# Row sums of layer 1 on GpSimd, norm statistics under the score products, the last biases in a convolution's sums

## The chip, the cores and the metric

The kernel runs on one core of a Trainium2 chip (trn2). The metric is the device time of one execution in microseconds. Times without a profile are from plain runs; the profile comes from one execution of its own, which takes a little longer, and its records are what the views below are made from.

## The reference

Two attention blocks stand one after the other on eight images of 512 channels by 32 x 32 pixels, all in fp32. Block 0 has 8 heads of 64 channels, block 1 a single head of 512 channels. A group norm stands before each block (32 groups and 8 groups), a residual sum behind it. Cut to what matters:

```python
# x: (8, 512, 32, 32) -> per image 512 channels x 1024 tokens
h = group_norm(x, gn_weight, gn_bias)                 # block 0, 32 groups
qkv = einsum('oc,bct->bot', w_qkv, h) + b_qkv
q, k, v = 8 heads of 64 channels each
weight = softmax(einsum('bct,bcs->bts', q * s, k * s), axis=-1)
a = einsum('bts,bcs->bct', weight, v)
x = x + einsum('oc,bct->bot', w_proj, a) + b_proj

xn = group_norm(x, gamma, beta)                       # block 1, 8 groups
q, k, v = conv1x1(xn, q_w, q_b), conv1x1(xn, k_w, k_b), conv1x1(xn, v_w, v_b)
attn = softmax(einsum('bqc,bck->bqk', q, k) / sqrt(512), axis=-1)
out = einsum('bqk,bkc->bqc', attn, v)
x = x + conv1x1(out, p_w, p_b)
```

## The kernel before

**Algebra.** Once, at the start, the kernel multiplies block 1's weights together: `m` from its q and k weights, `z` from its v and projection weights. Block 1 then needs one convolution with `m` (its result is called g), scores g times h, and a by-token product with `z`. Most matrix products are done in Winograd's form of Strassen's scheme: operands are cut into quarters, sums of quarters ("factors") are made on VectorE or GpSimd, TensorE does seven products in place of eight, and the results are put together with a few adds. `left_sums` and `right_sums` make the factors; `ORDER` is 1, 5, 2, 6, 7, 3, 4. Block 1's scores and the convolutions of `k`, `q` and `m` use the scheme twice, one inside the other: `inner_factors` and `query_factors` make the inner factors on GpSimd.

**One inner product.** `inner_steps` runs the seven inner products, its steps, in the order 1, 6, 2, 5, 7, and leaves steps 3 and 4 in the list `tail`, which runs (through `finish`) after step 1 of the next product. Each step is a small burst of matmuls into one of three pools of PSUM banks a, b and c, two buffers each. After step 1 ScalarE copies psa into psb. Step 6 leaves u2 (printed u), step 5 leaves c5 (printed c), and steps 2, 7, 3 and 4 end in an add by `add` on VectorE that reads PSUM and writes a quarter of the result. If a product is the first to write its quarters, ScalarE copies in place of some of these. After each step one item of the list `background` is put into the program, more at other places. TensorE's instructions, and others under `keep_in_program_order`, stay in the order in which the program gives them; the rest is ordered by the scheduler, engine by engine. Each engine then works through a queue of its own in order, and waits at an instruction until all that it needs is there.

**The order of work.** For each image b: attention of block 0 (`attention0`), its projection with the residual sum (`projection`), then block 1 of the image before: `layer1_scores` (the convolution with `m`), `layer1_rest` (scores, z, values), then values, keys and queries of image b+1 for block 0. Block 1 of images 0 to 6 takes the scores with inner factors (`scores1_twice`); the last image takes `scores1`, which is not touched. One such round takes some 355 us.

**The convolution, `conv2`.** Four pairs of outer products: (1, 5), (2, 6), (7), (3, 4), each with its seven inner steps. `blocks` names quarters of the result by (row, column). `add` puts a PSUM bank into one or two quarters. In the pair with product 7 `more` adds quarters on GpSimd. `biased_half` adds the bias to a quarter with two ACTIVATEs of ScalarE; it runs for (0, 0) after pair 1, for (1, 1) after pair 2, and for (1, 0) and (0, 1) after pair 3, or, for `q`, in the list `late`, which the main loop puts under the attention that follows. A `k` convolution has no bias here.

**The scores, `scores1_twice`.** Seven outer products, numbered 0 to 6 here as in the code (they are products 1, 2, 5, 6, 7, 3, 4 of the scheme). The scores are kept in eight tiles `e`, by column c, half cc and row r. Outer product 4 (number 7 of the scheme) belongs to three quarters: its steps put PSUM into one quarter, and `more` adds quarters to each other on GpSimd, eight adds of 128x512 elements (line 715). When a quarter is complete, `exps` takes its exponential on ScalarE, 128x1024 elements at a time (line 719). `add_up` sums exponentials for the softmax: `parts[r]` gets the sum over column and half, six adds of 128x1024 on VectorE (lines 724 and 726, printed sum<-e,e and sum<-sum,e), and `total` gets the sum of its two halves on GpSimd (line 727).

**Statistics.** `projection` leaves a list `stats` of twelve items: for each of the image's four x tiles two `bn_stats` on half a tile, 128x512 (line 98), and one `bn_aggr` (line 103). Four of its items go into `background` in the convolution of the image before (through a hook of pair 1), five at the start of outer product 0 of the scores, after g's first two sums (`gsteps`), the rest at outer product 2. The group means are needed in z (`norm_hooks`). All big tiles, x, e and the sums among them, come from one pool of 32 buffers, so when a tile is last read decides when a later load or a later tile can have its place.

Of the kernel before, what the change touches and what calls it, by code (L numbers as in the profile page):

```python
# [12 lines left out]
ALU = mybir.AluOpType  # L13
# [16 lines left out]
def two_attention_blocks_kernel(  # L30
# [41 lines left out]
    def pcols(name):  # L72
        i = 4 * PARAMS.index(name)
        return par[:, i : i + 4]
# [101 lines left out]
    def main_path(ctx):  # L176
# [318 lines left out]
            tail.extend([lambda: step(3), lambda: step(4)])  # L495
            tail.extend(final)

        def conv2(n, f, bias, name, hooks=(), after=(), late=None):

            out = channel_tiles(name)
            hooks = list(hooks)

            def blocks(places, r, cc):

                if len(places) == 2 and places[0][0] == places[1][0] and places[0][1] < places[1][1]:
                    t = out[2 * places[0][0] + r].rearrange("p (c q n) -> p c q n", c=2, q=2)  # L510
                    return [t[:, :, cc, :]]
                return [
                    out[2 * i + r].rearrange("p (c q n) -> p c q n", c=2, q=2)[:, c : c + 1, cc, :] for i, c in places
                ]

            def add(dst, ps, x):

                n = max(len(dst), len(x))
                for i in range(n):
                    d = dst[i] if len(dst) == n else dst[0][:, i : i + 1, :]  # L520
                    nc.vector.tensor_add(d, ps[:, i : i + 1, :] if n > 1 else ps, x[i] if len(x) == n else x[0][:, i : i + 1, :])  # L521
# [12 lines left out]

            def pair(s, products, y, x, final):
                w = weights2[s // 2][:, (0, 2, 0, 1)[s] :]

                def mm(ps, j, start):
                    for i, p in enumerate(products):
                        matmul(ps[:, i, :], w[:, i, j - 1, :], f[p][j], start=start and i == 0, stop=True, skip_group_check=True)  # L540

                def extra(r, cc, read, written):
                    if products == (7,):
                        if read:
                            more((0, 1), (0, 1), (1, 1), r, cc)
                        if written:
                            more((1, 1), (1, 0), (1, 1), r, cc)

                inner_steps(
                    f"{name}_{s}", s % 2, len(products), mm, add, lambda *at: blocks(y, *at), x and (lambda *at: blocks(x, *at)),  # L550
                    extra, hooks.pop(0) if hooks else (), final,
                )

            weights2 = [weight_part((n, 0))]
            pair(0, (1, 5), [(1, 0), (1, 1)], None, [])
            pair(1, (2, 6), [(0, 0), (0, 1)], [(1, 0), (1, 0)], [load_weight, lambda: biased_half(0, 0)])
            weights2.append(weight_part((n, 1)))
            pair(2, (7,), [(1, 0)], [(0, 1)], [lambda: biased_half(1, 1)])
            last = [lambda: biased_half(1, 0), lambda: biased_half(0, 1)]
            if late is not None:  # L560
                late += last
                last = []
            pair(3, (3, 4), [(0, 1), (1, 0)], [(0, 1), (1, 0)], [load_weight, *last, *after])
            return out


# [126 lines left out]
        def scores1_twice(b, f, gf, gsteps, first, uid, stats):  # L693
# [14 lines left out]
            def blocks(at, r, cc):  # L708
                return [e[at[1], cc, at[0]][:, :, ts(r, 2 * P)]]
# [1 line left out]
            def add(dst, ps, x):  # L711
                nc.vector.tensor_add(dst[0], ps, x[0])  # L712

            def more(dst, x, y, r, cc):
                nc.gpsimd.tensor_tensor(blocks(dst, r, cc)[0], blocks(x, r, cc)[0], blocks(y, r, cc)[0], ALU.add)  # L715

            def exps(r, c):
                for cc in (1, 0):
# [1 line left out]

            def add_up(r, c):

                if r == c:
                    return [lambda: nc.vector.tensor_add(parts[r], e[c, 0, r], e[c, 1, r])]
                return [
                    *(lambda cc=cc: nc.vector.tensor_add(parts[r], parts[r], e[c, cc, r]) for cc in range(2)),
                    lambda: nc.gpsimd.tensor_tensor(total[:, r, :], parts[r][:, 0, :], parts[r][:, 1, :], ALU.add),
                ]

            def product(s, p, y, x, before, small, after7=(), final=()):  # L730
                def mm(ps, j, start):
                    for i in range(2):
                        matmul(
                            ps[:, i, :], f[p][j][:, ts(i, P)], g2[p][j], start=start and i == 0, stop=True, skip_group_check=True
                        )

                def extra(r, cc, read, written):
                    if p == 7:
                        if read:
                            more((0, 1), (0, 1), (1, 1), r, cc)  # L740
                        if written:
                            more((1, 1), (1, 0), (1, 1), r, cc)

                inner_steps(
                    f"{uid}_{s}", s % 2, 2, mm, add, lambda *at: blocks(y, *at), x and (lambda *at: blocks(x, *at)),
                    extra, after7, final, [lambda: background.extend(small), *(lambda q=q: factors(q) for q in before)],
                )

# [242 lines left out]
        def keys_and_queries(b, f, norm, hooks):  # L991

            k = conv2("k", f, None, f"k0_{b}", hooks)
            hooks = [[all_background], [], []]
            if norm:
                hooks[1].append(lambda: norm.group_mean(acc_tile(f"gmean_0_{b + 1}")[:, :KC]))
                hooks[2].append(lambda: norm.affine(acc_tile(f"gvar_0_{b + 1}")[:, :KC]))
            late = []
            q = conv2("q", f, pcols("bq0"), f"q0_{b}", hooks, late=late)
            return q, k, late  # L1000

        def layer1_scores(b, hf, inner, hooks=()):
            if inner:
# [37 lines left out]
        for b in range(B):  # L1041
# [17 lines left out]

            if b > 0:  # L1060
                hf, t = image_factors(h, f"h1_{b - 1}", here)
                extra[0] += late
# [13 lines left out]
            if b > 0:  # L1076
# [14 lines left out]
                if b + 1 < B:  # L1091
                    hf, steps = image_factors(h, f"h0_{b + 1}")
                    background.extend(steps)
                    v, f, norm0 = values(b + 1, hf)
                    q, k, late = keys_and_queries(b + 1, f, norm0, ())
            elif B > 1:
                v, f, norm0 = values(1, hf, [[], [], [], [], [*steps[:7], scaled, steps[7]]])
                norm1, stats = projection(0, af, xt)
                hooks = norm_hooks(norm1, "1_0")
                hooks[0].append(lambda: background.extend(stats))  # L1100
                q, k, late = keys_and_queries(1, f, norm0, hooks)
            else:
                for f in (*steps[:7], scaled, steps[7]):
                    f()
# [209 lines left out]
```

## Time and profile before

| | |
|---|---|
| Median of three plain runs | 2902.51 us (2902.0 to 2902.94) |
| The profiled execution | 2908.49 us |
| Its span in the profile | 2906.6 us |
| Mean granted TensorE clock | 0.994 |
| TensorE matmuls (PE) busy | 2852.4 us, 98% |
| TensorE weight loads (PEld) busy | 1678.3 us, 58% |
| VectorE (DVE) busy | 2098.9 us, 72% |
| GpSimd (POOL) busy | 1018.8 us, 35% |
| ScalarE (ACT) busy | 953.8 us, 33% |
| DMA, mean over the span | 97 GB/s |

The span runs from the first to the last instruction of the profile; the execution's time has a little more around it. Weight loads lie under matmuls. In the views a line such as `psb L67 <- DVE e L712: 29.8, 21, 3.7` says that TensorE, at its instructions into psb of line 67, waited 29.8 us in all, 21 times and at most 3.7 us, for VectorE's instruction of line 712 with the output e. A line of a timeline gives the start in us from the start of the span, the time from start to end, the engine, the line of the code, the operation, its output and inputs by the program's names, and the tile; several of a kind in a row are drawn together (x4). Brackets at its end say how long the engine was kept waiting before it, and by whom. A line of windows gives a stretch of time, its length, and then, for TensorE's matmuls and loads, VectorE, ScalarE, GpSimd and SyncE, the busy us (and the number of instructions), and last TensorE's clock, the DMA engines' busy share and GB/s.

### The profile page before, as it was taken

To read this page: it belongs to the slowest core of one execution; us is meant where nothing else is said; L and a number is where in the kernel's file an instruction comes from. 1 tells how busy PE (TensorE), PEld (TensorE's weight loads), DVE (VectorE), ACT (ScalarE), POOL (GpSimd) and SP (SyncE) were. 2 spreads that over 40 slices of the span, in tenths; PEclk is the share of its full clock that TensorE was granted. 3 is DMA by queue.
4 is the path that set the end of the run, shared out by engine and by line. 5 is a ranking of instruction groups with operands and counts; after the bars stand their busy time and mean duration, and the time that the engine had idled before them with its cause. 6 is when DMAs were issued, how large, how long until landed. Compare 5 with 4: busy or idle time off the path is not lost.

```text
span 2906.6 us, 32039 instructions
## 1 busy us (share of the span) xinstructions
PE 2852.4 (98%) x11720; PEld 1678.3 (58%) x11720; DVE 2098.9 (72%) x2760; ACT 953.8 (33%) x1222; POOL 1018.8 (35%) x1068
## 2 busy tenths in 40 slices
PE   9999999999999999999999999999999999999998
PEld 5435636765367653767437674376733768347544
DVE  5587787667876678775787667877588775887654
ACT  1351453215522055221642216431163312633110
POOL 2113226532164322742227412365124551145200
PEclk9999999999999999999999999999999999999999
DMA  8722403133032221322212231122411224021201
GB/s 274 245 91 105 155 19 141 52 116 125 33 124 87 98 108 48 109 92 104 102 48 105 92 135 70 48 105 95 153 53 48 102 102 149 21 81 68 94 0 67
DMA packets 91595, 281.03 MB, mean 97 GB/s; under 512 B 10595, under 2 KB 36387, under 8 KB 82470
## 3 DMA queue, kind: packets, MB, share of 16 engines
q1 hardware_dynamic: 89638, 276.61, 26.2%
q10 hardware_dynamic: 1792, 2.29, 0.2%
q8 instruction: 95, 1.56, 0.2%
q14 instruction: 70, 0.57, 0.1%
HBM read 225.93 MB, written 52.93 MB: 96 GB/s over the span
## 4 chain that ended last, share of the span: by engine, by line
PE 90%; DVE 4%; POOL 3%; issue 1%; ACT 1%; DMA 0%; SPq 0%; DVEq 0%; POOLq 0%; ACTq 0%
PE sc L67 16%; PE av L67 15%; PE psb_av L67 5%; PE psa_av L67 4%; PE psc_av L67 4%; PE psb L67 4%; PE psb_z L67 3%; PE psb_p L67 3%; PE psb_v L67 3%; PE psb_k L67 3%; PE psb_g L67 2%; PE psb_q L67 2%; POOL e L715 2%; PE psa_p L67 2%; PE psa_z L67 2%; PE psc_v L67 2%
## 5 line engine op out<-in xcount | busy, mean ns | idle before, releaser
L617 DVE TENSOR_TENSOR sum<-sum,e 128x1024 f32<-128x1024 f32 x384 | 519.3, 1352 | 41.8 <-DVE sum L617 1.8
L613 ACT ACTIVATE e<-sc 128x1024 f32<-128x1024 f32 x512 | 476.8, 1053 | 72.2 <-PE sc L67 72.2
L67 PE MATMUL sc<-q,k 64*128 64x512 f32 x2048 | 458.4, 597 | 0.0
L67 PE MATMUL av<-e,v 128*64 128x512 f32 x2048 | 453.6, 596 | 0.0
L67 PEld LDWEIGHTS sc<-q,k 64*128 64x128 f32 x2048 | 193.5, 186 | 238.1 <-ACT e L613 105.2
L67 PEld LDWEIGHTS av<-e,v 128*64 128x64 f32 x2048 | 141.4, 137 | 304.3 <-issue 302.3
L580 POOL TENSOR_TENSOR all_recs<-all_recs,rc 128x256 f32<-128x256 f32 x72 | 63.6, 884 | 567.7 <-DVE rc L578 560.1
L636 POOL TENSOR_TENSOR a<-a,r 128x512 f32<-128x512 f32 x56 | 116.7, 2083 | 263.5 <-DMA r<-rows 258.7
L578 DVE RECIPROCAL rc<-sums 128x256 f32<-128x256 f32 x72 | 126.5, 1757 | 48.0 <-PE sums L67 26.9
L631 ACT COPY a<-av 128x512 f32<-128x512 f32 x64 | 37.4, 585 | 305.6 <-PE av L67 305.6
L526 POOL TENSOR_TENSOR k<-k,k 128x256 f32<-128x256 f32 x28 | 20.1, 726 | 319.7 <-DVE u_k L521 319.7
L615 DVE TENSOR_TENSOR sum<-e,e 128x1024 f32<-128x1024 f32 x64 | 78.4, 1225 | 59.6 <-ACT e L613 59.6
L67 PE MATMUL psa_av<-e,z 128*128 128x512 f32 x256 | 113.3, 596 | 0.0
L67 PE MATMUL psb<-inner,inner_h 128*128 128x256 f32 x392 | 106.5, 397 | 0.0
L140 ACT ACTIVATE h<-h,b,s 128x1024 f32<-128x1024 f32 x62 | 78.3, 1268 | 80.4 <-DMA h<-in_x 64.9
L411 POOL TENSOR_TENSOR inner_h<-h,inner_h 128x256 f32<-128x256 f32 x112 | 95.8, 858 | 2.2
L411 POOL TENSOR_TENSOR inner_h<-t_h 128x256 f32<-128x256 f32 x84 | 85.0, 1015 | 17.9 <-PE psc_av L67 15.4
L67 PEld LDWEIGHTS psb<-inner,inner_h 128*128 128x128 f32 x392 | 78.2, 200 | 11.5
L719 ACT ACTIVATE e<-e 128x1024 f32<-128x1024 f32 x56 | 58.4, 1055 | 77.4 <-POOL e L715 42.0
L67 PE MATMUL psb_g<-inner_h,w_m 128*128 128x256 f32 x294 | 75.2, 384 | 6.3 <-DVE u_g L521 6.3
L67 PEld LDWEIGHTS psa_av<-e,z 128*128 128x128 f32 x256 | 48.1, 190 | 57.2 <-issue 56.5
L715 POOL TENSOR_TENSOR e<-e,e 128x512 f32<-128x512 f32 x56 | 69.9, 1268 | 21.3 <-DVE u L712 19.7
(374 smaller groups left out, 5438.8 us busy)
## 6 DMA issues: line engine op xcount, KB each, us to landing
x<-in_x SPq DMA_DIRECT2D x36, 512.0 KB
h<-in_x SPq DMA_DIRECT2D x32, 512.0 KB
spill<-x SPq DMA_DIRECT2D x32, 512.0 KB
h<-spill SPq DMA_DIRECT2D x32, 512.0 KB
x<-spill SPq DMA_DIRECT2D x32, 512.0 KB
out<-x SPq DMA_DIRECT2D x64, 256.0 KB
w_p<-sums_p SPq DMA_DIRECT2D x8, 1792.0 KB
r<-rows SPq DMA_DIRECT2D x112, 128.0 KB
```

The costliest lines, as they stand in the source:

```text
L67: tc.keep_in_program_order(nc.tensor.matmul(*args, **kw))
L140: tc.keep_in_program_order(nc.scalar.activation(dst, src, AF.Identity, bias=b, scale=s))
L411: pin(nc.gpsimd.tensor_tensor(dst, x, y, ALU.subtract))
L578: nc.vector.reciprocal(rc, sums)
L580: nc.gpsimd.tensor_tensor(all_recs, all_recs, rc, ALU.add)
L613: nc.scalar.activation(e, sc, AF.Exp, scale=(C // 8) ** -0.5)
L615: nc.vector.tensor_add(total, es[0], e)
L617: nc.vector.tensor_add(total, total, e)
L631: nc.scalar.copy(dst, av)
L636: nc.gpsimd.tensor_tensor(dst, dst, r, ALU.mult)
L715: nc.gpsimd.tensor_tensor(blocks(dst, r, cc)[0], blocks(x, r, cc)[0], blocks(y, r, cc)[0], ALU.add)
L719: nc.scalar.activation(e[c, cc, r], e[c, cc, r], AF.Exp, scale=scale)
```

## The change

It has four parts.

**Biases.** The halves (1, 0) and (0, 1) of a biased convolution (`q` and `m`) are no longer biased by ScalarE after pair 3. The adds of pair 3 that write them become a `scalar_tensor_tensor` each (PSUM plus bias plus the old quarter). `late` is gone. The halves (0, 0) and (1, 1) stay with ScalarE.

**Row sums.** The six adds of `add_up` on e go from VectorE to GpSimd, and all sums are pinned to the order of the program on GpSimd.

**Adds of outer product 4.** Of the eight `more` adds of `scores1_twice` two go from GpSimd to VectorE: the read one at (r, cc) = (0, 1), and the written one at (1, 0).

**Statistics.** None is in the convolution with `m` any more. The twelve items stand in outer products 0 (three, ahead of g's first sums), 3 (three, behind the first row sum), 4 (one), 5 (three) and 6 (two, ahead of row sums).

```diff
@@ conv2
-        def conv2(n, f, bias, name, hooks=(), after=(), late=None):
+        def conv2(n, f, bias, name, hooks=(), after=()):
...
                     d = dst[i] if len(dst) == n else dst[0][:, i : i + 1, :]
-                    nc.vector.tensor_add(d, ps[:, i : i + 1, :] if n > 1 else ps, x[i] if len(x) == n else x[0][:, i : i + 1, :])
+                    psi = ps[:, i : i + 1, :] if n > 1 else ps
+                    xi = x[i] if len(x) == n else x[0][:, i : i + 1, :]
+                    if isinstance(d, tuple):
+                        d, oc = d
+                        nc.vector.scalar_tensor_tensor(d, psi, bias[:, oc : oc + 1], xi, ALU.add, ALU.add)
+                    else:
+                        nc.vector.tensor_add(d, psi, xi)
...
             def pair(s, products, y, x, final):
+                def written(r, cc):
+                    to = blocks(y, r, cc)
+                    if s < 3 or bias is None:
+                        return to
+                    return [(t, 2 * i + r) for t, (i, _) in zip(to, y)]
...
-            last = [lambda: biased_half(1, 0), lambda: biased_half(0, 1)]
-            if late is not None:
-                late += last
-                last = []
-            pair(3, (3, 4), [(0, 1), (1, 0)], [(0, 1), (1, 0)], [load_weight, *last, *after])
+            pair(3, (3, 4), [(0, 1), (1, 0)], [(0, 1), (1, 0)], [load_weight, *after])
@@ scores1_twice
-            def more(dst, x, y, r, cc):
-                nc.gpsimd.tensor_tensor(blocks(dst, r, cc)[0], blocks(x, r, cc)[0], blocks(y, r, cc)[0], ALU.add)
+            def more(engine, dst, x, y, r, cc):
+                engine.tensor_tensor(blocks(dst, r, cc)[0], blocks(x, r, cc)[0], blocks(y, r, cc)[0], ALU.add)
...
             def add_up(r, c):
+                on = lambda dst, x, y: lambda: tc.keep_in_program_order(nc.gpsimd.tensor_tensor(dst, x, y, ALU.add))
                 if r == c:
-                    return [lambda: nc.vector.tensor_add(parts[r], e[c, 0, r], e[c, 1, r])]
+                    return [on(parts[r], e[c, 0, r], e[c, 1, r])]
                 return [
-                    *(lambda cc=cc: nc.vector.tensor_add(parts[r], parts[r], e[c, cc, r]) for cc in range(2)),
-                    lambda: nc.gpsimd.tensor_tensor(total[:, r, :], parts[r][:, 0, :], parts[r][:, 1, :], ALU.add),
+                    *(on(parts[r], parts[r], e[c, cc, r]) for cc in range(2)),
+                    on(total[:, r, :], parts[r][:, 0, :], parts[r][:, 1, :]),
                 ]
...
                         if read:
-                            more((0, 1), (0, 1), (1, 1), r, cc)
+                            more(nc.vector if (r, cc) == (0, 1) else nc.gpsimd, (0, 1), (0, 1), (1, 1), r, cc)
                         if written:
-                            more((1, 1), (1, 0), (1, 1), r, cc)
+                            more(nc.vector if (r, cc) == (1, 0) else nc.gpsimd, (1, 1), (1, 0), (1, 1), r, cc)
...
-            product(0, 1, (1, 0), None, [2], gsteps[:2] + stats[:5])
+            product(0, 1, (1, 0), None, [2], stats[:3] + gsteps[:2])
             product(1, 2, (0, 0), (1, 0), [5], gsteps[2:4], (), [lambda: exps(0, 0)])
-            product(2, 5, (1, 1), None, [6, 4], gsteps[4:] + stats[5:])
-            product(3, 6, (0, 1), (1, 0), [7, 3], add_up(0, 0))
-            product(4, 7, (1, 0), (0, 1), [], [])
-            product(5, 3, (0, 1), (0, 1), [], [], [lambda: exps(1, 1)], [lambda: exps(0, 1)])
+            product(2, 5, (1, 1), None, [6, 4], gsteps[4:])
+            product(3, 6, (0, 1), (1, 0), [7, 3], add_up(0, 0) + stats[3:6])
+            product(4, 7, (1, 0), (0, 1), [], stats[6:7])
+            product(5, 3, (0, 1), (0, 1), [], stats[7:10], [lambda: exps(1, 1)], [lambda: exps(0, 1)])
             product(
-                6, 4, (1, 0), (1, 0), [], add_up(1, 1) + add_up(0, 1), (),
+                6, 4, (1, 0), (1, 0), [], stats[10:] + add_up(1, 1) + add_up(0, 1), (),
                 [lambda: exps(1, 0), lambda: background.extend(add_up(1, 0) + steps)],
             )
@@ main loop
-                gf, gsteps = layer1_scores(b - 1, hf, inner, [[], [lambda: background.extend(stats[:4])]])
+                gf, gsteps = layer1_scores(b - 1, hf, inner)
...
-                layer1_rest(b - 1, hf, inner, gf, gsteps, stats[4:], [[], mean, [], affine], ahead)
+                layer1_rest(b - 1, hf, inner, gf, gsteps, stats, [[], mean, [], affine], ahead)
```

More of the change, by code (lines that the diff above doesn't have):

```diff
@@ L540, in mm, with extra @@
                         matmul(ps[:, i, :], w[:, i, j - 1, :], f[p][j], start=start and i == 0, stop=True, skip_group_check=True)
-                def extra(r, cc, read, written):
+                def extra(r, cc, read, done):
                     if products == (7,):
@@ L545, in extra @@
                             more((0, 1), (0, 1), (1, 1), r, cc)
-                        if written:
+                        if done:
                             more((1, 1), (1, 0), (1, 1), r, cc)
                 inner_steps(
-                    f"{name}_{s}", s % 2, len(products), mm, add, lambda *at: blocks(y, *at), x and (lambda *at: blocks(x, *at)),
+                    f"{name}_{s}", s % 2, len(products), mm, add, written, x and (lambda *at: blocks(x, *at)),
                     extra, hooks.pop(0) if hooks else (), final,
@@ L997, in keys_and_queries @@
                 hooks[2].append(lambda: norm.affine(acc_tile(f"gvar_0_{b + 1}")[:, :KC]))
-            late = []
-            q = conv2("q", f, pcols("bq0"), f"q0_{b}", hooks, late=late)
-            return q, k, late
+            q = conv2("q", f, pcols("bq0"), f"q0_{b}", hooks)
+            return q, k
         def layer1_scores(b, hf, inner, hooks=()):
@@ L1061, in main_path @@
                 hf, t = image_factors(h, f"h1_{b - 1}", here)
-                extra[0] += late
                 for i, fs in enumerate((t[:1], t[1:2], (t[2], t[4]), (t[6], t[3]), (t[5], t[7]), steps[:2], steps[2:4])):
@@ L1094, in main_path @@
                     v, f, norm0 = values(b + 1, hf)
-                    q, k, late = keys_and_queries(b + 1, f, norm0, ())
+                    q, k = keys_and_queries(b + 1, f, norm0, ())
             elif B > 1:
@@ L1100, in main_path @@
                 hooks[0].append(lambda: background.extend(stats))
-                q, k, late = keys_and_queries(1, f, norm0, hooks)
+                q, k = keys_and_queries(1, f, norm0, hooks)
             else:
```

## The prediction

> **What bounds the kernel now.** I read the engine shares first, then TensorE's own waits, then the timelines of TensorE, VectorE and GpSimd around the longest of them.
>
> ```profile
> PE 2852.4 (98%) x11720; PEld 1678.3 (58%) x11720; DVE 2098.9 (72%) x2760; ACT 953.8 (33%) x1222; POOL 1018.8 (35%) x1068
> ...
> PE psb L67 <- DVE e L712: 29.8, 21, 3.7
> PE psb_g L67 <- DVE u_g L521: 6.3, 7, 0.9
> ...
> PE psc L67 <- ACT c L449: 1.2, 7, 0.2
> ```
>
> TensorE is the bound: 54.2 us of the 2906.6 us span are idle, and only waits that TensorE itself sits in are worth anything. The repeated ones occur 7 times: layer 1 with inner factors runs once for each of images 0 to 6. VectorE's, ScalarE's and GpSimd's shares mean nothing by themselves.
>
> ```profile
> 532.01 1.03 PE L67 MATMUL psc<-inner,h 128*128 128x256 f32 x4
> 536.76 2.08 PE L67 MATMUL psb<-sg,inner_h 128*128 128x256 f32 x4 [3.72 <-DVE e L712]
> 538.62 1.76 PE L67 MATMUL psb<-inner,inner_h 128*128 128x256 f32 x4
> 540.23 1.03 PE L67 MATMUL psa<-g,t_h 128*128 128x256 f32 x4
> ...
> 523.54 10.21 POOL L715 TENSOR_TENSOR e<-e,e 128x512 f32<-128x512 f32 x8 [2.80 <-DVE u L712]
> ...
> 530.56 0.69 DVE L712 TENSOR_TENSOR c<-psc,e 128x512 f32<-128x512 f32 x1 [0.17 <-PE psc L67]
> 534.88 1.23 DVE L724 TENSOR_TENSOR sum<-e,e 128x1024 f32<-128x1024 f32 x1 [3.63 <-ACT e L719]
> 536.02 0.68 DVE L712 TENSOR_TENSOR e<-psb,c 128x512 f32<-128x512 f32 x1
> ...
> 536.70:539.00 2.30, 2.24 (x5) 1.85 (x6) 0.73 (x3) 1.06 (x1) 0.00 (x0) 0.50 0.00 0
> ```
>
> Read upwards: TensorE's step 4 of score product 5 waits for VectorE's read of psb at 536.02. That read was ready at 531.3, but stood in VectorE's queue behind the row sum of L724, which waited for an exponential, which waited for the eight L715 adds on GpSimd (523.54 to 533.75). After the gap TensorE runs at clock 0.50 (last line, the first of its last three figures, which are clock, DMA share and GB/s; before them stand sum and mean of each engine's busy time): five steps take 6.06 us to 542.82 instead of 5 x 0.8635 = 4.32. Over the seven images the gap costs 3.89 us each beyond the pipelined pace and the slow clock another 15.0 us in all.
>
> ```profile
> 486.28 0.68 DVE L98 BATCH_NORM_STATS2 bnst<-x 128x6 f32<-128x512 f32 x1
> 486.88 0.41 DVE L521 TENSOR_TENSOR u_g<-psb_g,g 128x256 f32<-128x256 f32 x1
> 487.43 0.67 PE L67 MATMUL psb_g<-inner_h,w_m 128*128 128x256 f32 x2 [0.89 <-DVE u_g L521]
> ```
>
> Here a statistics instruction stands ahead of the read that TensorE waits for.
>
> **What the Trainium skill says.** "TensorE: Matmul & The Clock Gate" (What's actually happening): about one idle window of 3.4 us halves the clock; the trace agrees (3.72 us idle, then 0.50). The same page (Architectural detail) calls VectorE's queue strictly first in, first out; agrees, see 534.88. "GPSIMD Engine Reference" (4.1 Engine selection): two-input operations about twice VectorE's time; agrees, L765 on 128x1024 takes 2.44 us on GpSimd against 1.22 on VectorE. "SBUF — State Buffer" (SBUF: two separate sides): a GpSimd operation and a VectorE one with two SBUF inputs exclude each other. The trace agrees: the 128x4 subtraction of L117 took 1.26 us beside L727, while L712, which reads PSUM, keeps 0.69 us beside L715.
>
> **The change, part by part** (per image, on the profiled execution; the orders are those of the built program; TensorE's and the DMA queue's are the same in both).
>
> *A, convolution without statistics.* Four bn_stats leave the `m` convolution. The step at 487.43 was due at 485.94 + 0.43 = 486.37, so it lost 1.06. Without the statistics of 485.03 and 486.28 the two g<-psb_g run from 485.3, u_g ends at 486.4, TensorE starts at 486.46: **-0.97**.
>
> *Biases.* Four ACTIVATEs of 0.72 us leave ScalarE per biased convolution; eight 128x256 adds become scalar_tensor_tensor. By L945 against L238 (0.738 against 0.692 for 128x512, both from PSUM) that is about 0.03 us each, 0.24 us on VectorE. In the last pair TensorE had no wait on VectorE, so nothing on the path. For `q` the late activations lay under attention, where the second half's first scores began without a gap (345.92 = 331.04 + 7.29 + 7.02 + 0.57): 0. The price if VectorE's slack were gone is 0.24.
>
> *B, start of the scores, products 0 to 2.* From 493.25 to 509.56 TensorE lost 0.34 + 0.55 + 0.11 + 0.09 + 0.47 + 0.10 = 1.66 us, waiting for ScalarE's c copy (behind the bias activations) and VectorE's first reads (behind sg and statistics). Afterwards c ends at 499.24 and the first read at 500.2, before TensorE's 501.0. The statistics are only three, ahead of that read, under matmuls. But the sg and g sums now stand between VectorE's reads, and collide with GpSimd's inner factors (0.68 becomes 0.9 to 1.2 in the trace): step 4 of product 1, due 507.05, is read at 507.4 or later. I leave 0.4 to 1.0 of the 1.66, and take **-1.0** (bounds -0.6 and -1.5).
>
> *C, product 3.* Statistics were moved here. The x tiles are now freed later, and the built order is u, c, bn_stats, e<-psa, bn_stats, e<-psb,c, where it was u, e<-psa, c, e<-psb,c. c can't start before 518.40; then 0.6 each for the four (back-to-back pace of the 0.69 us rows): e<-psb,c runs from 520.8 to 521.5. Step 4 was due at 520.79: **+0.76**. Bounds 0 (the profile's dues are a little early) and +0.8.
>
> *D, the long stall.* The row sum leaves VectorE, so the wait of 534.88 leaves with it; what is late next? Two of the eight adds go to VectorE and six stay. Call the start of step 6 of product 4 t0 (before: 521.65).
> - VectorE: u at t0+1.12, its add 1.72, a bn_stats 2.32, e<-psa 2.92 to 3.61. GpSimd's first add overwrites what e<-psa reads, so it starts at t0+3.69; before, GpSimd began at t0+1.89.
> - Six adds at 10.21/8 = 1.276: end at t0+11.34 (before, eight: t0+12.10).
> - VectorE's second add, which stands in product 5 behind u, overwrites the half of e that GpSimd's sixth add reads. It waits to t0+11.4, and VectorE's queue with it: then 0.6 each for add, e<-psa and bn_stats; c from 13.2 to 13.89.
> - TensorE's step 3 of product 5 needs c read: t0+13.95 instead of t0+10.37. Step 4 follows at 14.81; before, at 15.11.
>
> So the stall moves one step earlier and stays: **-0.30**. The gap is 3.4 us instead of 3.72, about the skill's window, so I keep the slow clock's cost; without it up to another -2.1. Bounds -0.8 and +0.5.
>
> *Row sums on GpSimd.* Six 128x1024 adds of 2.44 us, 14.7 us per image. The first must end before t0+3.69: the inner factors ended at 520.74, t0-0.91, then 2.5, so 2.1 us of room, more because GpSimd no longer waits 1.84 for the biased g at 498.24. The last two can start after the exponential at 550.1: 2 x 2.44 + 1.27 end at 556.4 instead of 554.88. TensorE's sums matmul is due at 562.35: 6 us of cover. They block VectorE's small d, d2, dv and the t sums by about 1.3 us (564.15 to 565.5); TensorE needs w_z's reads at 569.89. The reciprocal's row transfers and the loads of x and h queued behind them on SP move by the same 1.3 us; ScalarE waits for h at 581.3, TensorE uses it after 604. All 0; if this cover were gone it would be 1.3.
>
> Sum: -0.97 - 1.0 + 0.76 - 0.30 = -1.5 us, times 7 = -10.6 us. The profiled execution took 2908.49 us (span 2906.6 and 1.9 around it): 2897.9. The median shown is 2902.51, 6 us lower, so **2892 us**.
>
> **Rivals.**
> 1. *The stall goes away.* The row sum that the stall hung on leaves VectorE; if the second add did not hold VectorE, all 3.89 and the clock's 15.0/7 = 2.14 would go: (-1.21 - 6.03) x 7 = -51, **2852 us**. Against it: the add must not overwrite before GpSimd's sixth has read.
> 2. *The places only swap.* VectorE's queue stays full, sg sums and locks eat B, and D is +0.3: -0.97 + 0 + 0.76 + 0.3 = +0.1, **2903 us**. For it: a lock wait of 0.3 to 0.5 on two sums does it.
> 3. *Slower: the first row sum holds the adds.* It stands in GpSimd's queue right before the six adds. Should it end after t0+3.69, every microsecond lengthens the stall. From 1.5 us late on the gain is used up; from 2.3 on it is slower by 0.2%. With the locked 3.25 us of the e<-e,e row of L765 and inner factors 3 us later it ends at t0+6.1, 2.4 late: +0.9 x 7, **2909 us**. Against it: in the trace GpSimd idles 2.80 us right there.
>
> **How the numbers follow.** Likeliest 0.66 (own range 2882 to 2897), rival 1 0.05, rival 2 0.18, rival 3 0.11. The range 2879 to 2905 takes in the likeliest with its bounds and rival 2, and leaves out rival 1 and rival 3's larger part. 0.2% (5.8 us) is about what a measurement can tell from none. Faster by more than that: rival 1 and nearly all of the likeliest, 0.69; within: rival 2 and a rim of the likeliest, 0.20; slower 0.11.
>
> **What would show it.** A: TensorE's wait on u_g gone. B: at most 1 us lost in the first 16 us of the scores. C: a new wait of about 0.7 us on psb, two products before the long one. D: VectorE idle some 2 us before a 128x512 add of e, released by GpSimd; TensorE's long gap about 3.4 us, now ahead of psc. If VectorE does not wait there, or GpSimd's adds start far from t0+3.7, the prediction is wrong.

## The result

| | median | runs | ratio to before, 95% interval |
|---|---|---|---|
| before | 2902.51 us | 2901.64 to 2904.36 (13) | |
| after | 2896.62 us | 2894.23 to 2899.84 (13) | 0.998 (0.9971 to 0.9988) |

The kernel after is 5.9 us faster, 0.2%. The forecast was 10.5 us, with 2879 to 2905 as range. All figures are of undisturbed executions: of the ten in the experiment with the statistics alone, two took 3064.77 and 8132.13 us and are left out. The profiled execution of the kernel after took 2894.85 us with a span of 2893.1. Here is part 1 of its page, and then, in a second fence, the waits of TensorE (line, what it waited for, us in all, times, longest). Line 720 of the kernel after is line 712 of the one before, line 723 is 715, line 727 is 719, and line 731 holds the row sums.

```profile
PE 2847.5 (98%) x11720; PEld 1669.2 (58%) x11720; DVE 2069.1 (72%) x2732; ACT 919.8 (32%) x1166; POOL 1092.1 (38%) x1096
```

```profile
PE psc L67 <- DVE mv L103: 24.2, 7, 3.7
PE psb L67 <- DVE e L720: 5.0, 7, 0.7
```

Of the three kinds of wait of before, those on u_g and on ScalarE's c are gone. The long gap has moved from psb to psc and is still there seven times. A new wait of 0.7 us on psb has come.

The timeline around the long gap of image 0, TensorE first, then GpSimd, then VectorE:

```profile
529.98 1.03 PE L67 MATMUL psa<-g,t_h 128*128 128x256 f32 x4
534.41 1.50 PE L67 MATMUL psc<-inner,h 128*128 128x256 f32 x4 [3.41 <-DVE mv L103]
535.71 1.91 PE L67 MATMUL psb<-sg,inner_h 128*128 128x256 f32 x4
...
524.11 7.64 POOL L723 TENSOR_TENSOR e<-e,e 128x512 f32<-128x512 f32 x6 [3.43 <-issue]
...
527.65 0.69 DVE L720 TENSOR_TENSOR u<-psb,e 128x512 f32<-128x512 f32 x1 [0.24 <-PE psb L67]
531.78 0.69 DVE L723 TENSOR_TENSOR e<-e,e 128x512 f32<-128x512 f32 x1 [3.44 <-POOL e L723]
532.39 0.68 DVE L720 TENSOR_TENSOR e<-psa,e 128x512 f32<-128x512 f32 x1
533.00 0.68 DVE L98 BATCH_NORM_STATS2 bnst<-x 128x6 f32<-128x512 f32 x1
533.60 0.67 DVE L720 TENSOR_TENSOR c<-psc,e 128x512 f32<-128x512 f32 x1
534.18 0.20 DVE L103 BATCH_NORM_AGGREGATE mv<-bnst 128x2 f32<-128x12 f32 x1
```

VectorE's queue stands for 3.44 us at its second add (531.78), which GpSimd's sixth add releases. Behind it lie e<-psa, a statistic and c, the read that frees psc. TensorE starts at 534.41, 0.14 us after c ended. The profile names the bn_aggr of 534.18 as releaser, since it came last before the start; c is what psc waited for.

**Where the time went.** I take TensorE's pace of 0.8635 us per step and add up, step by step, what each start is late (the same count that gave 1.66 us in the prediction; a gap counted so is 0.17 us longer than the idle time in brackets, 3.58 for 3.41):

| per image | before | after | forecast | measured |
|---|---|---|---|---|
| A: first matmul of the m convolution to first of the scores | 27.55 | 26.70 | -0.97 | -0.85 |
| B: late in outer products 0 to 2 | 1.66 | 0.88 | -1.0 | -0.78 |
| C: late in outer product 3 | 0 | 0.98 | +0.76 | +0.98 |
| late in outer product 4 | 0 | 0.24 | 0 | +0.24 |
| D: the long gap | 3.90 | 3.58 | -0.30 | -0.32 |
| sum | | | -1.5 | -0.73 |

Seven images make 5.1 us less. The biases cost 0.05 us at the end of each q convolution and 0.12 at the attention behind it, in seven images (not six, as the expectations below put it): 1.2 us more. That leaves 3.9 us. The rest is the slow stretch, the time behind a gap in which TensorE runs at a lower clock: it costs 1.69 us per image where it follows (from the resumption to the first matmul of z 6.94 us with it and 5.25 without). In the kernel before it follows every gap, in the kernel after five of seven in this execution, so up to 3.4 us more: 3.9 to 7.3, with the measured 5.9 between. The plain runs of the kernel after spread over 5.6 us, about three such stretches.

Two windows of the kernel after, of images 3 and 2, show it; after the engines' busy time come clock, DMA share and GB/s. Both follow a gap of 3.58 us, with a clock of 1.00 in the one and 0.64 in the other:

```profile
1598.30:1602.60 4.30, 4.29 (x20) 3.81 (x21) 3.40 (x6) 2.00 (x2) 1.94 (x2) 1.00 0.00 0
1243.77:1248.10 4.33, 4.32 (x13) 3.58 (x14) 2.04 (x3) 2.00 (x2) 1.59 (x1) 0.64 0.00 0
```

The new wait of C, product 3 of image 0, in the timeline:

```profile
516.62 0.68 DVE L98 BATCH_NORM_STATS2 bnst<-x 128x6 f32<-128x512 f32 x1
517.34 0.69 DVE L720 TENSOR_TENSOR e<-psa,e 128x512 f32<-128x512 f32 x1
517.95 0.68 DVE L98 BATCH_NORM_STATS2 bnst<-x 128x6 f32<-128x512 f32 x1
518.55 0.67 DVE L720 TENSOR_TENSOR e<-psb,c 128x512 f32<-128x512 f32 x1
...
519.28 1.13 PE L67 MATMUL psb<-sg,inner_h 128*128 128x256 f32 x4 [0.71 <-DVE e L720]
```

Two statistics stand ahead of e<-psb,c, as the built order said; step 4 is 0.88 us late, and the step behind it 0.10 more.

### The profile page after: what moved, and what is told of

The parts are those of the page before. It is cut to its first block, busy times and chain, and to the rows that moved or that the text cites. A ratio compares the mean times of both kernels' runs of the same rounds, so it can differ in the third digit from the quotient of the medians.

```text
span 2893.1 us, 31974 instructions
## 1 busy us (share of the span) xinstructions
PE 2847.5 (98%) x11720; PEld 1669.2 (58%) x11720; DVE 2069.1 (72%) x2732; ACT 919.8 (32%) x1166; POOL 1092.1 (38%) x1096
## 4 chain that ended last, share of the span: by engine, by line
PE 93%; issue 2%; DVE 2%; POOL 2%; DMA 0%; SPq 0%; ACT 0%; DVEq 0%; POOLq 0%
PE sc L67 16%; PE av L67 16%; PE psb_av L67 6%; PE psa_av L67 4%; PE psc_av L67 4%; PE psb L67 3%; PE psb_z L67 3%; PE psb_p L67 3%; PE psb_v L67 3%; PE psb_g L67 3%; PE psb_k L67 3%; PE psb_q L67 2%; PE psc L67 2%; PE psa_p L67 2%; PE psa_z L67 2%
## 5 line engine op out<-in xcount | busy, mean ns | idle before, releaser
L731 POOL TENSOR_TENSOR sum<-sum,e 128x1024 f32<-128x1024 f32 x28 | 65.9, 2354 | 43.5 <-ACT e L727 42.4
L411 POOL TENSOR_TENSOR inner_h<-h 128x256 f32<-128x256 f32 x56 | 54.3, 969 | 66.7 <-ACT h L140 66.7
L411 POOL TENSOR_TENSOR inner_h<-t_h 128x256 f32<-128x256 f32 x84 | 74.0, 884 | 12.9 <-PE psc_av L67 8.8
```

The lines of the kernel that those rows point to most:

```text
L411: pin(nc.gpsimd.tensor_tensor(dst, x, y, ALU.subtract))
L731: on = lambda dst, x, y: lambda: tc.keep_in_program_order(nc.gpsimd.tensor_tensor(dst, x, y, ALU.add))
```

## The experiments

The theory: the gap follows VectorE's second add, hence GpSimd's sixth, and the moved statistics lengthen it. Rivals are named run by run. Ratios are to the kernel before on the same chip; it ran at 2902.7, 2906.2 and 2903.2 us (medians) beside the three groups of runs below.

### Both kernels again

The two profiles first taken differ by 13.6 us, more than twice the medians. So both kernels ran again, unchanged.

> The kernel before, unchanged, for a second profile. The first profiled execution (2908.49 us) lies 6 us above the median of the plain runs, and the two profiles differ by 13.6 us where the medians differ by 5.9. Theory: part of that is chance of the one profiled execution: two of seven images had 0.4 and 1.3 us more of slow clock after the long gap, and four images a wait of 0.47 us on w_av that the kernel after does not show. Then this profile shows those extras on other images or on fewer of them, and comes out 2 to 6 us shorter. Rival: they belong to the kernel's order; then the four waits on w_av stand on the same images and the span is again within 1 us of 2906.6.

> The kernel after, unchanged, for a second profile and for times on the same chip as the next two. Plain runs of it fall into two groups, near 2894.5 and near 2898.3 us. Theory: the long gap of 3.57 us is close to what the clock needs to fall, and whether the slow stretch of 1.77 us follows is decided image by image; in the first profile it followed in five of seven. So the gap is 3.4 to 3.7 us on all seven images again, the slow stretch follows in five to seven, and the time differs from 2894.85 by 1.75 us for each image more. Rival: the groups come from something else (transfers at the start), then the number of slow stretches is again five whatever the time.

The second profile of the kernel before has a span of 2901.9 us (execution 2903.68), 4.7 below the first. One line of its waits:

```profile
PE psb_av L67 <- DVE w_av L238: 0.5, 1, 0.5
```

The wait on w_av stands there once, where the first profile had it four times (1.9 us, each 0.73 to 0.77 with the delay behind it); and one image, not two, has an overlong slow stretch (7.3 us to z where the others have 6.0 to 6.1; in the first profile 7.35 and 7.41, so they were 1.2 and 1.3 us over, not 0.4 and 1.3). Three waits less make 2.2 us, one overlong stretch less 1.3, and TensorE's first waits for weights at the start of the kernel 1.2: together the 4.7 us. The kernel is the same, so these are chance of one execution. A profiled execution does not take longer as such: this one took 2903.68 us where the plain median beside it is 2902.66. What lies behind the wait on w_av is shown in the last section.

The kernel after came to 2896.71 us (18 runs, ratio 0.9981, 0.9974 to 0.9988). Its gap is again 3.58 to 3.60 us (3.88 in image 1); five slow stretches again, but on other images: image 2 lost its own, image 3 gained one. The profiled time, 2895.47, is 0.6 us above the first with the same number of stretches. So the theory of the count agrees, but with five stretches in both profiles a change of the count was not seen. The mean clock of each of the 31 runs of this kernel points the same way: the seven with 0.997 took 2894.37 to 2896.62 us, the five with 0.994 took 2898.44 to 2899.84.

### The last add back on GpSimd

```diff
-                            more(nc.vector if (r, cc) == (1, 0) else nc.gpsimd, (1, 1), (1, 0), (1, 1), r, cc)
+                            more(nc.gpsimd, (1, 1), (1, 0), (1, 1), r, cc)
```

> The kernel after with one edit: the last of the eight adds of outer product 4, which the change gave to VectorE, goes back to GpSimd (seven there, one on VectorE). Theory: in the kernel after VectorE's queue stands at this add for 3.44 us because it must not overwrite what GpSimd's sixth add still reads; without it e<-psa and c are read at once and TensorE's gap ahead of psc is gone. What is late next is ScalarE: its exponential of the quarter now needs GpSimd's seventh add (about 533.0 in the time of image 0), and the copy psa to psb of product 6 stands behind it (done about 534.7), so TensorE waits about 2.2 us at psb of product 6 in place of 3.57: 1.4 us less per image, 10 us in all, and up to 1.77 us more per image if the clock does not fall after 2.2 us: 2874 to 2887 us. Rival 1: GpSimd's adds as such are too late for VectorE's reads; then the gap stays at psc, as long as before, 2896. Rival 2: the bn_aggr which the profile names as releaser of psc, and the bn_stats, hold the queue; then the gap stays too.

2879.97 us, ratio 0.992 (0.9906 to 0.9934), 16.7 us below the kernel after. Its waits, and in a second fence its timeline:

```profile
PE psb L67 <- ACT psb L459: 14.0, 7, 2.0
```

```profile
530.74 1.06 ACT L727 ACTIVATE e<-e 128x1024 f32<-128x1024 f32 x1 [5.24 <-POOL e L723]
533.33 1.06 ACT L727 ACTIVATE e<-e 128x1024 f32<-128x1024 f32 x1 [1.53 <-POOL e L723]
534.29 0.58 ACT L459 COPY psb<-psa 128x512 f32<-128x512 f32 x1
...
534.92 1.56 PE L67 MATMUL psb<-inner,inner_h 128*128 128x256 f32 x4 [2.03 <-ACT psb L459]
```

No wait on psc is left, though the bn_aggr and the statistics stand where they did: both rivals fall. What is late next is ScalarE, as worked out: the gap is 2.19 us where 2.2 was expected (1.96 in image 6). The slow stretch follows on two images of seven.

### ScalarE's copy ahead of the waiting exponentials

```diff
-                    nc.scalar.copy(ps["b"], ps["a"])
+                    (tc.keep_in_program_order if early else (lambda i: i))(nc.scalar.copy(ps["b"], ps["a"]))
...
-                    nc.scalar.activation(e[c, cc, r], e[c, cc, r], AF.Exp, scale=scale)
+                    tc.keep_in_program_order(nc.scalar.activation(e[c, cc, r], e[c, cc, r], AF.Exp, scale=scale))
...
-            product(5, 3, (0, 1), (0, 1), [], stats[7:10], [lambda: exps(1, 1)], [lambda: exps(0, 1)])
+            product(5, 3, (0, 1), (0, 1), [], stats[7:10], [], [lambda: exps(1, 1), lambda: exps(0, 1)])
```

The first two edits pin copy and exponentials to the program's order, which the third changes.

> As the run with the last add on GpSimd, and ScalarE's copy psa to psb of product 6 stands ahead of the two exponentials that wait for GpSimd, not behind them (these exponentials run after steps 3 and 4 of product 5). Theory: nothing of TensorE's path waits for the adds of outer product 4 any more; the long gap goes away altogether, and the slow clock with it: 3.57 us times seven and 1.77 us times five or seven, 34 to 37 us below the kernel after, 2859 to 2863 us. The row sums end about as before, some 7 us ahead of the matmul that needs them. Rival: the gap was only cover for something right behind it (GpSimd's sum of the row, a read of e that needs the sixth add at step 4); then half of it comes back within the next product and the time is 2875 or more.

This stands on top of the edit before it. 2862.26 us, ratio 0.986 (0.9845 to 0.9875). The largest of TensorE's waits, and the timeline of ScalarE and GpSimd:

```profile
PE psb L67 <- DVE e L720: 5.0, 7, 0.7
```

```profile
530.44 0.57 ACT L459 COPY psb<-psa 128x512 f32<-128x512 f32 x1 [5.71 <-PE psa L67]
...
523.51 9.03 POOL L723 TENSOR_TENSOR e<-e,e 128x512 f32<-128x512 f32 x7 [3.43 <-issue]
...
547.61 1.27 POOL L731 TENSOR_TENSOR sum<-sum 128x512 f32<-128x512 f32 x1
```

The copy runs while GpSimd is still adding. The largest wait that remains is that of C. The long gap is gone and does not come back anywhere; the clock never falls after it. GpSimd's last sum ends at 548.88, 6.1 us ahead of the matmul on it (554.96), which is the cover that the prediction gave the row sums.

### Each part alone

On the kernel before: the biases alone, the statistics' new places alone, the row sums on GpSimd alone, and the row sums with the split of the eight adds (the diff of the change, cut to these parts).

> The kernel before with the biases alone (the last halves in the adds of pair 3, late gone). Theory: ScalarE's c copies in outer products 0 and 1 are no longer behind bias activations, so about half of the 1.66 us lost there comes back (0.8 per image), and the wider adds cost 0.05 us at the end of q and 0.12 at the first scores of attention (as the kernel after shows) in six images: 0.8 x 7 - 0.17 x 6 = 4.6 us less, 2898 us (2895 to 2902). Rival: the loss in the first products is VectorE's (sums of g, statistics), not ScalarE's; then nothing comes back and the time is 2903.5.

> The kernel before with the new places of the statistics alone; row sums on VectorE, all eight adds on GpSimd. Theory: the m convolution gains 0.85 us per image, outer product 3 loses 0.9, the start of the scores gains some 0.3, and the long gap stays at 3.9 with its slow clock, since its row sum still waits for the same exponential: 0.25 x 7 = 2 us less, 2901 us (2898 to 2905). Rival: statistics in outer products 4 and 5 lengthen the long gap themselves; then it is 4.5 us and the time 2905 or more.

> The kernel before with the row sums on GpSimd alone; the eight adds all stay on GpSimd, the statistics where they were. Theory: VectorE no longer waits for an exponential, so the gap at psb of product 5 is gone; late next is ScalarE, whose copy for product 6 stands behind the exponential that needs the eighth add (533.75): exponential to 534.86, copy to 535.43, where TensorE is due at 533.76: a gap of 1.75 us in place of 3.89, and after so short a gap the slow stretch (1.77 us) follows on two images or fewer, as after 2.19 us in the run with the last add back on GpSimd. 15 + 9 = 24 us less: 2879 us (2874 to 2886). Rival: GpSimd's row sum pushes the eight adds back by its 2.4 us; then the gap is 4 us again and the time 2903 or more.

> The kernel before with the row sums on GpSimd and two of the eight adds on VectorE; statistics and biases as before. Theory: VectorE's second add waits for GpSimd's sixth, as in the kernel after, but no statistics stand ahead of e<-psa in product 4 (0.6 us, which starts GpSimd's adds) and ahead of c in product 5 (0.6 us): the gap is about 2.4 us in place of 3.58, too short for the clock in most images: 1.5 x 7 + 9 = 19 us less than before, 2883 us (2878 to 2890), so 13 us faster than the whole change. Rival: the gap hangs on the split alone; then it is 3.4 to 3.6 us as in the whole change, with its slow stretches, and the time 2898 to 2901.

| | median us | ratio (95%) | late in products 0 to 2, us | late in product 3, us | gap, us | slow stretches |
|---|---|---|---|---|---|---|
| biases | 2904.02 | 0.9994 (0.9986 to 1.0002) | 1.23 | 0 | 3.89 | 6 of 7 |
| statistics | 2898.57 | 0.9976 (0.9966 to 0.9986) | 0.75 | 0.98 | 3.91 | 5 of 7 |
| row sums | 2875.71 | 0.9897 (0.9882 to 0.9911) | 1.65 | 0 | 1.68 | 0 of 7 |
| row sums and split | 2886.50 | 0.9936 (0.9923 to 0.9949) | 1.65 | 0 | 2.65 | 3 of 7 |

The row sums alone are worth 30 us, five times the whole change. Their timeline:

```profile
519.01 2.37 POOL L723 TENSOR_TENSOR sum<-e,e 128x1024 f32<-128x1024 f32 x1
522.87 10.23 POOL L715 TENSOR_TENSOR e<-e,e 128x512 f32<-128x512 f32 x8 [1.50 <-DVE u L712]
...
534.10 0.58 ACT L459 COPY psb<-psa 128x512 f32<-128x512 f32 x1
...
534.73 1.13 PE L67 MATMUL psb<-inner,inner_h 128*128 128x256 f32 x4 [1.50 <-ACT psb L459]
```

GpSimd's row sum ends 1.50 us before the eight adds can start, so it pushes nothing back; the rival falls. With all eight adds on GpSimd only ScalarE is late.

With the split GpSimd ends sooner (six adds, 7.65 us), but VectorE is held by its own add:

```profile
523.69 7.65 POOL L715 TENSOR_TENSOR e<-e,e 128x512 f32<-128x512 f32 x6 [2.90 <-DVE e L712]
...
531.37 0.69 DVE L715 TENSOR_TENSOR e<-e,e 128x512 f32<-128x512 f32 x1 [3.10 <-POOL e L715]
...
533.41 1.10 PE L67 MATMUL psc<-inner,h 128*128 128x256 f32 x4 [2.48 <-DVE c L712]
```

So the split gives back 11 of the 30 us, and its rival falls: the gap without the statistics is 2.65 us, not 3.4 to 3.6.

The sizes were missed on three of the four. The row sums were expected to save 24 us: the gap is as worked out (1.68 for 1.75), but no slow stretch at all follows, worth 3.4 us more than two; what is left, about 3 us, I can't place. (In this group of runs the kernel before took 3.5 us longer than in the first, with a mean clock of 0.994 in 18 of 23 runs against 7 of 22; the profile of the biases alone has two overlong slow stretches, 7.45 and 7.20 us to z. More of these in the kernel before would explain the rest; that is not shown.) The statistics saved 7.6 us where 2 were expected: B is 0.91 us per image and not 0.3, so A, B and C make 0.78, 5.5 in all; two gaps without a slow stretch would more than cover the rest. The biases saved 2.2 us where 4.6 were expected, and the interval takes in no change: 0.43 per image and not 0.8, less their 1.2 us. And the two gains at the start of the scores don't add: with both, the kernel after loses 0.88 us there, no less than with the statistics by themselves.

### The kernel after, with the statistics of products 4 and 5 later

```diff
-            product(4, 7, (1, 0), (0, 1), [], stats[6:7])
-            product(5, 3, (0, 1), (0, 1), [], stats[7:10], [lambda: exps(1, 1)], [lambda: exps(0, 1)])
+            product(4, 7, (1, 0), (0, 1), [], [])
+            product(5, 3, (0, 1), (0, 1), [], [], [lambda: exps(1, 1)], [lambda: exps(0, 1)])
             product(
-                6, 4, (1, 0), (1, 0), [], stats[10:] + add_up(1, 1) + add_up(0, 1), (),
+                6, 4, (1, 0), (1, 0), [], stats[6:] + add_up(1, 1) + add_up(0, 1), (),
```

> The kernel after with one edit: the four statistics items of outer products 4 and 5 go to product 6, ahead of the two there. Theory: in the kernel after, the statistic ahead of e<-psa in product 4 starts GpSimd's six adds 0.6 us later, and the one ahead of c in product 5 keeps TensorE 0.6 us longer once VectorE goes on; without them the long gap is that of the run with row sums and split alone, 2.65 us and not 3.58, the wait of 0.24 us in product 4 goes too, and the slow stretch follows on about three images and not five to seven: (0.94 + 0.24) x 7 + 3 x 1.77 = 13.5 us less than the kernel after, 2883 us (2878 to 2888). Rival: the gap of 3.58 comes from the biases or from product 3's later end; then it stays at 3.5 or more and the time is 2894 to 2897.

2881.77 us, ratio 0.9925 (0.9911 to 0.9938). From its waits:

```profile
PE psc L67 <- DVE c L720: 17.6, 7, 2.8
```

The gap is 2.65 us (2.93 in image 1), nothing is late in product 4, and the slow stretch follows three gaps. So the two statistics ahead of e<-psa and of c are worth 0.93 us of gap per image, and with the 0.24 us of product 4 and the clock about 15 us in all.

### Both repairs together, without and with the biases

Row sums and all eight adds on GpSimd, the copy ahead of the exponentials, and of the change's places for the statistics all but product 3's, which go behind the sums of g in product 2:

```diff
-            product(2, 5, (1, 1), None, [6, 4], gsteps[4:])
-            product(3, 6, (0, 1), (1, 0), [7, 3], add_up(0, 0) + stats[3:6])
+            product(2, 5, (1, 1), None, [6, 4], gsteps[4:] + stats[3:6])
+            product(3, 6, (0, 1), (1, 0), [7, 3], add_up(0, 0))
```

> The kernel before with the row sums on GpSimd, all eight adds there too, the new places of the statistics except that product 3's three items stand in product 2 behind the sums of g, and ScalarE's copy for product 6 ahead of the two exponentials. Theory: against the run with the exponentials late (2862.3) the 0.98 us at product 3 and the 0.24 at product 4 go, and the biases' 0.17 us in six images: 9.5 us less, 2853 us (2849 to 2857); TensorE's waits in the scores are then those of the first three products alone, some 0.8 us per image. Rival: three statistics more in product 2 cost there what they cost in product 3; then 2859 to 2861.

> As the run before it in this list, with the biases part of the change added. Theory: beside the moved statistics the biases bring nothing (0.75 us lost in the first three products with the statistics alone, 0.88 in the kernel after) and cost 0.17 us in six images: 1 to 2 us slower than without them, 2854 us. Rival: they bring the 0.43 us per image of the run with biases alone; then 2 us faster than without them.

2852.92 us without the biases, ratio 0.9827 (0.9813 to 0.984), and 2854.97 with them, 0.9834 (0.982 to 0.9847), each within 1 us of what was expected; both rivals fall. TensorE's largest waits without them:

```profile
PE tr_wk L70 <- DMA rawk<-in_w: 3.8, 1, 3.8
PE psb_av L67 <- DVE w_av L238: 1.6, 2, 0.8
PE psc L67 <- POOL inner L426: 1.2, 7, 0.2
```

No repeated wait above 0.2 us is left in the scores; 0.76 us per image is late in products 0 to 2 and 0.24 in product 3. With the biases products 0 to 2 lose 0.88. The 2.05 us between the two is what 0.12 and 0.17 us in seven images make (2.0). The two intervals overlap, but no run of the one lies among the runs of the other (2852.43 to 2854.01 and 2854.1 to 2855.67).

## Why the prediction was right or wrong

- **A** held: -0.85 for -0.97. TensorE starts the step that was 1.06 us late at 485.81, still 0.2 us after its due (485.17 + 0.43), where 0.09 was put down.
- **B** held within its bounds, -0.78 for -1.0. Its reason was half wrong: the gain comes with the statistics. The biases' share (0.43 alone) is not added on top of it. What is left stands behind the sums, as forecast: two sg sums beside GpSimd's inner factors take 2.03 us where two others beside an idle GpSimd take 1.28, the read of u behind them ends at 502.98, and TensorE's step 7 starts at 503.13, 0.28 late.
- **C** was undersized: +0.98 for +0.76. The wait is the one worked out, 0.88 us late, but VectorE, once late, is 0.10 late for the step behind it too.
- **Product 4** was missing from the sum. Its own statistic makes TensorE 0.24 us late there; the prediction followed it only as far as GpSimd's start.
- **Biases** at 0 were wrong. The cover named, first scores without a gap, has none to give to the convolution's last adds, which write what they read: a scalar_tensor_tensor takes 0.48 us where the add took 0.42 (0.06 more, where 0.03 was put down), 0.12 for the last two, and attention's first stretch of scores is 0.12 us longer. The profile of the biases alone has the same 0.12 on all seven images. With the 0.05 in q that is 1.2 us in all; per image, 0.17, it lies inside the price of 0.24 given if VectorE's slack were gone.
- **D** held to 0.2 us at every station. With t0 = 520.24, the start of step 6 of product 4: GpSimd starts at t0 + 3.87 (forecast 3.69) and ends at t0 + 11.51 (11.34), VectorE's add starts at t0 + 11.54 (11.4), c ends at t0 + 14.03 (13.89) and step 3 starts at t0 + 14.17 (13.95). The sign named for it, VectorE idle some 2 us, does not fit these stations: u of product 5 was to end at t0 + 7.9, so the wait to t0 + 11.4 comes to 3.5; it is 3.44.
- **The slow clock** was kept at its full cost; two gaps of seven went without it, 3.4 us in this execution. That part of the 5.9 us is luck for the forecast: with a slow stretch behind every gap about 3.9 would be left.
- **Rival 1**, that the stall goes, needs the second add not to hold VectorE. It does, so the rival fell; with that hold and ScalarE's behind it taken away the time was 2862. **Rival 3**, GpSimd's row sum too late for the adds, fell: it ended 3.43 us before them. **Rival 2** was the nearest of the three in size, but not by its own reasons: B and D came nearly as put down, and C, product 4 and the biases took the gain.

The mechanism held; the sum is 4.6 us off. Its weak terms are the parts that add work to VectorE in front of TensorE's reads: C and product 4 cost 0.46 us per image more than put down, the biases 1.2 us in all, and A and B brought 0.34 per image less. The slow stretches that stayed away gave part of it back.

The larger lesson lies outside the forecast number. The row sums alone save 30 us; 11 go to the split, 15 to the statistics of products 4 and 5 by the runs with them moved. These shares do not add up: the same statistics cost 15 us with the split in place, and by themselves, on the kernel before, the new places saved 7.6; and the slow stretches come in whole pieces.

## What to carry to other kernels

When a blocking instruction is moved off an in-order queue, look at what else in the same change puts onto that queue a new instruction that waits for the same engine: here an add of 0.69 us, moved to relieve GpSimd, kept the queue waiting 3.44 us. Run the parts of a change alone; one may be worth several times the whole. And give filler work places by the slack of the reads behind it, not by the busy share of its engine: VectorE was at 72.2% before and 71.5% after, and two or three statistics of 0.68 us cost or saved up to 1.0 us of TensorE's time per image by where they stood.

## What the runs showed of the hardware

How often the slow clock follows a gap of TensorE, over the images of ten profiles:

| gap us | TensorE idle in it, us | images with a slow stretch |
|---|---|---|
| 1.68 | 1.50 | 0 of 7 |
| 2.19 (one of 1.96) | 2.03 | 2 of 7 |
| 2.65 (one of 2.93) | 2.48 | 6 of 14 |
| 3.58 (two of 3.88) | 3.41 | 10 of 14 |
| 3.90 | 3.73 | 25 of 28 |

The Trainium skill ("TensorE: Matmul & The Clock Gate", What's actually happening) has the clock fall after at least one idle window of 3.4 us, in windows that run freely. That the same gap is followed by a slow stretch on one image and not on the next agrees with free windows. But gaps of 2.19 us, which hold no idle window of 3.4, were followed by one on two images, and gaps of 3.90 not on three. Here the measurement decides: over these lengths the chance of a slow stretch rises with the gap, from none at 1.68 us to nearly all at 3.90, and shortening it from 3.9 to 2.2 or 1.7 us saved more in clock (8 to 12 us) than each microsecond of gap alone would have told.

The Trainium skill ("SBUF — State Buffer", SBUF: two separate sides) has GpSimd and a VectorE operation with two SBUF inputs lock each other out for a whole instruction. In the kernel after this reached a tiny instruction: beside GpSimd's last two row sums VectorE's product of 128x4 elements took 2.23 us where it takes 0.16 in the profile of before. The sum that needs it was ready at 553.68, 3.4 us ahead of the matmul on it (557.12), so it cost nothing.

In the kernel before, VectorE was held over several instructions of GpSimd, and that reached TensorE. These lines of the first profile of the kernel before are VectorE's product of o and r (two SBUF inputs) on image 0, what follows it, and the same product on image 2:

```profile
602.48 7.51 DVE L783 TENSOR_TENSOR o<-o,r 128x512 f32<-128x512 f32 x1
611.05 0.68 DVE L238 TENSOR_TENSOR w_av<-psb_av,t_av 128x512 f32<-128x512 f32 x1
611.78 2.41 PE L67 MATMUL psb_av<-t,z 128*128 128x512 f32 x5 [0.47 <-DVE w_av L238]
...
1315.41 1.07 DVE L783 TENSOR_TENSOR o<-o,r 128x512 f32<-128x512 f32 x1
```

In the 7.51 us GpSimd ran some ten operations of 128x256 back to back; on image 2 the same product took 1.07 us beside the same operations. In the 13 profiles this product took 7.5 to 7.8 us on 14 images of 91, and on these 14 alone TensorE waited 0.46 to 0.79 us for w_av. That the lock is what held it is read from the overlap; no run took these operations away.
